# A longer prefix ahead of the branch: three graph attentions, group 0's first layer and all weight folding around the scan

## The chip, the cores and the metric

The kernel runs on one core of a Trainium2 chip. Its metric is device time in microseconds for one execution. Beside the runs there is a profiled execution, from which the views of the profile and the trace come; its span runs from the first to the last instruction. Engines are named as in the profile: PE is TensorE (PEld its weight loads), DVE is VectorE, ACT is ScalarE, POOL is GpSimd, SP is SyncE, which here issues the DMAs.

## The reference

128 graphs of 128 nodes with 256 features go through two layers. All arithmetic is in 32-bit floats.

```python
# layer 0: two graph attentions, then a feed-forward layer (256 -> 1024 -> 256)
def _gat(h, adj, W, a, out_features):
    Wh = jnp.matmul(h, W)
    Wh1 = jnp.matmul(Wh, a[:out_features])
    Wh2 = jnp.matmul(Wh, a[out_features:])
    e = jax.nn.leaky_relu(Wh1 + jnp.swapaxes(Wh2, 1, 2), negative_slope=ALPHA)
    scores = jnp.where(adj > 0, e, NEG)
    att = jax.nn.softmax(scores, axis=1)
    return jnp.matmul(att, Wh)
h = _gat(x, adj, W1, a1, Fout)
h = _gat(h, adj, W2, a2, W2.shape[1])
h = _layernorm(residual + h, g_ln1, b_ln1)
ff = jnp.matmul(jax.nn.relu(jnp.matmul(h, w_ff1) + b_ff1), w_ff2) + b_ff2
x = _layernorm(h + ff, g_ln2, b_ln2)
# layer 1: 8-head attention with a value matrix per relation r = 0..3, then a feed-forward layer
attn = softmax(q k^T / sqrt(dh))
for r in range(4):
    out = out + einsum('bhij,bhjd->bhid', attn * (adj == r), v_r)
x = _ln(src + out @ Wo + bo, g1, beta1)
ff = gelu(x @ W1 + b1) @ W2 + b2
return _ln(x + ff, g2, beta2)
```

## The kernel before, in words

The graphs are taken in 32 groups of four. Each group goes through five stages: `load` (features and mask), `gat` (both graph attentions), `ff0` (layer 0's feed-forward), `att` (layer 1's attention) and `ff1` (layer 1's feed-forward). Each stage is a Python generator that emits instructions and yields a planned time until its next piece; a heap in `layers` always continues the generator with the earliest planned time, so the pieces of several groups are mixed. `PERIOD` (100 units of plan) is the distance between groups, `begin` gives the start of each stage in a period, `early` moves single stages, and `times` holds the pauses. From a planned time on (`kept`), the order of emission is binding for TensorE and for SP; the other engines are ordered by the scheduler of the build.

Work differs by whether a group goes "direct". A transpose is either made by TensorE against the identity, into PSUM, and copied out (L282 to L286; L406 for the row of a graph attention), or by VectorE in blocks of 32 (L288) with a trip through DRAM that puts the blocks into place (four stores L291, one load L297; for a row L411 and L414). Direct is meant for groups with little other work beside them: before, the two graph attentions in the prefix, `ff0` of group 0, the features of `att` for group 0, and `ff0`, `att` and `ff1` of the last group. The weights of `att` for group 0 take the trip through DRAM (`turned`).

The names in the steps: L442 is x times the folded weights (wh), L450 and L461 the weighted sums of the first and second graph attention, L424 to L431 their softmax. L315 to L318 and L339 form the first feed-forward product from sums of blocks (seven products for eight), in two units of four visits each; L345 to L366 evict and activate; L384 is the second feed-forward product. L476 and L481 are q and k, L497 the scores, L501 to L513 the softmax over heads, L548 the values, L532 masks the weights, L563 weights the values, L590 is the product with Wo. `affine` (L271) applies a layer norm's gain and offset, `normalised` (L256 to L265) its mean and variance. `folded` (L184, L192, L195) multiplies a layer norm's gain into the next weights and its offset into their bias, `weight_sums` (L208 to L212) prepares the sums of weight blocks.

The program begins with a prefix. It loads the first weights and two groups, does these groups' graph attentions side by side, step by step, scans the whole adjacency input for a value above 1 (four parts of 2 MB, L722), folds wf1, and brings a flag to a register:

```python
        while gats:
            gats = [s for s in gats if next(s, None) is not None]
...
    with tc.If(found > 0) as arm:
        layers(tc, a, out, c, GENERAL)
    with arm.Else():
        layers(tc, a, out, c, BINARY)
```

With the inputs used the adjacency holds only 0 and 1, so the second arm runs (two value sets in place of four). All engines pass the branch. In the arm, group 0's attention stage first folds wq, wk, wv and w1; the graph attention of group 2 and everything later belongs to the arm.

## Time and profile before

| | us |
|---|---|
| median of 3 runs | 2838.19 (2837.97 to 2843.73) |
| profiled execution, its own time | 2833.85 |
| its span | 2831.9 |
| TensorE busy | 2718.5 |
| ScalarE busy | 1679.3 |
| GpSimd busy | 1547.0 |
| VectorE busy | 1527.5 |
| granted TensorE clock, mean | 0.982 |

Busy is the sum of the instructions' times on an engine. In the page's second part each digit is the busy share of one of 40 slices of the span in tenths; PEclk is the granted TensorE clock in tenths. In a table of windows the columns after a window are its length, then for each engine the busy time and the number of instructions, then the granted clock, the busy share of the DMA engines and the traffic. In a list of waits each line has the engine with the instruction that waited, what released it, the total in us, how many times, and the longest.

### The profile page before, as it was taken

What the parts mean: (1) busy time and instruction counts of PE and PEld (TensorE: products, weight loads), DVE (VectorE), ACT (ScalarE), POOL (GpSimd) and SP (SyncE); (2) the same over time, 40 slices, a digit from 0 to 9 for tenths busy, and PEclk for the clock granted to TensorE, in tenths of its full rate; (3) what the DMA queues carried; (4) which work ended last, traced back from release to release, by engine and by line L of the source; (5) the groups of instructions that cost most, each with busy time, mean ns of one, the idle gap of its engine ahead of it and who ended that gap; (6) DMA issues with size and microseconds to landing.
All of it is one profiled execution on the core that took longest, in us unless ns stands there. A gap on an engine that the chain in (4) does not pass through costs nothing.

```text
span 2831.9 us, 46682 instructions
## 1 busy us (share of the span) xinstructions
PE 2718.5 (96%) x16578; PEld 2148.2 (76%) x16578; DVE 1527.5 (54%) x2873; ACT 1679.3 (59%) x5063; POOL 1547.0 (55%) x1610
## 2 busy tenths in 40 slices
PE   4897999999999999999999999999999999999888
PEld 3775877777787777787777778778778877777766
DVE  5445555555654555565555555555556555555442
ACT  3445656666665666665666565566666556566443
POOL 1434646555655655665564565565566556556453
PEclk7898999999999999999999999999999999999999
DMA  7146365556456556555555655655664555565220
GB/s 281 46 100 143 83 134 112 111 128 142 105 115 133 112 107 139 118 120 121 119 113 119 142 108 113 137 109 108 135 133 108 118 124 117 110 142 108 63 51 15
DMA packets 1156945, 328.74 MB, mean 116 GB/s; under 512 B 903008, under 2 KB 1126752, under 8 KB 1156064
## 3 DMA queue, kind: packets, MB, share of 16 engines
q1 hardware_dynamic: 1156704, 325.68, 52.0%
q8 instruction: 133, 2.18, 0.3%
q14 instruction: 108, 0.88, 0.1%
HBM read 195.97 MB, written 129.62 MB: 115 GB/s over the span
## 4 chain that ended last, share of the span: by engine, by line
PE 62%; ACT 11%; DVE 10%; DMA 6%; POOL 5%; issue 4%; SPq 1%; ACTq 0%; DVEq 0%; POOLq 0%
PE mm L384 23%; PE mm L339 16%; PE mm L548 4%; PE mm L476 4%; DMA eT<-zd 4%; PE mm L481 4%; ACT e L510 3%; PE av L563 3%; ACT fT L360 2%; PE mm L590 2%; DVE nm L501 2%; ACT tok L265 2%; PE mm L497 2%; POOL e L513 2%; PE mm L450 2%
## 5 line engine op out<-in xcount | busy, mean ns | idle before, releaser
L271 POOL TENSOR_TENSOR tok<-tok,ln_rows 128x512 f32<-128x512 f32 x476 | 616.9, 1312 | 25.4 <-DVE T L288 8.1
L510 ACT ACTIVATE e<-mm,nm 128x128 f32<-128x128 f32 x1024 | 358.5, 402 | 203.9 <-DVE nm L501 201.5
L384 PE MATMUL mm<-w,fT 128*128 128x256 f32 x2048 | 463.8, 382 | 0.0
L384 PE MATMUL mm<-wf,fT 128*128 128x256 f32 x2048 | 448.7, 379 | 1.5 <-ACT fT L360 1.5
L384 PEld LDWEIGHTS mm<-wf,fT 128*128 128x128 f32 x2048 | 388.7, 190 | 55.4 <-ACT fT L360 1.9
L384 PEld LDWEIGHTS mm<-w,fT 128*128 128x128 f32 x2048 | 384.2, 190 | 59.4 <-issue 6.0
L532 DVE TENSOR_TENSOR m<-eT,am 128x1024 f32<-128x1024 f32 x128 | 183.9, 1437 | 404.6 <-DMA eT<-zd 403.9
L513 POOL TENSOR_TENSOR e<-e,s 128x1024 f32<-128x1024 f32 x128 | 254.4, 1994 | 133.7 <-DVE s L512 118.4
L265 ACT ACTIVATE tok<-tok,nmr,rstd 128x256 f32<-128x256 f32 x480 | 251.0, 608 | 117.9 <-POOL nmr L263 117.7
L431 POOL TENSOR_TENSOR e<-e,s 128x512 f32<-128x512 f32 (+1 forms) x68 | 68.0, 1000 | 455.7 <-DVE s L430 455.6
L315 POOL TENSOR_TENSOR t<-T 128x256 f32<-128x256 f32 x64 | 48.2, 753 | 450.9 <-DMA T<-zd 450.9
L429 ACT ACTIVATE e<-e,nm 128x128 f32<-128x128 f32 x256 | 99.6, 390 | 298.3 <-DVE nm L426 292.0
L510 ACT ACTIVATION_READ_ACCUMULATOR e<-mm,nm 128x1 f32 x1024 | 247.8, 242 | 0.0
L548 PE MATMUL mm<-wv,T 128*128 128x512 f32 x512 | 230.2, 592 | 0.0
L358 POOL TENSOR_TENSOR fT<-fT 128x512 f32<-128x512 f32 x128 | 161.1, 1269 | 86.7 <-ACT fT L357 86.6
L339 PE MATMUL mm<-T,wf 128*128 128x256 f32 x768 | 197.4, 381 | 0.0
L339 PE MATMUL mm<-T,w 128*128 128x256 f32 x768 | 194.4, 382 | 0.3 <-ACT T L286 0.2
L360 ACT ACTIVATE fT<-fT,col 128x512 f32<-128x512 f32 x256 | 167.8, 711 | 29.9 <-DVE fT L354 29.4
L256 DVE BATCH_NORM_STATS2 st<-tok 128x6 f32<-128x256 f32 x480 | 179.8, 412 | 4.1
L394 DVE TENSOR_TENSOR tok<-tok,mm 128x512 f32<-128x512 f32 x120 | 81.8, 681 | 182.7 <-PE mm L384 182.7
L339 PEld LDWEIGHTS mm<-T,w 128*128 128x128 f32 x768 | 147.1, 192 | 35.6 <-issue 15.5
L548 PEld LDWEIGHTS mm<-wv,T 128*128 128x128 f32 x512 | 97.1, 190 | 95.1 <-issue 87.5
(141 smaller groups left out, 5140.2 us busy)
## 6 DMA issues: line engine op xcount, KB each, us to landing
zd<-e SPq DMA_DIRECT2D x496, 128.0 KB, 3.6
eT<-zd SPq DMA_DIRECT2D x124, 512.0 KB, 5.1
zd<-T SPq DMA_DIRECT2D x364, 128.0 KB, 3.6
T<-zd SPq DMA_DIRECT2D x91, 512.0 KB, 4.4
xt<-in_xT_dram SPq DMA_DIRECT2D x32, 512.0 KB, 5.3
e<-zsd SPq DMA_DIRECT2D x60, 256.0 KB, 3.2
tok<-in_x_dram SPq DMA_DIRECT2D x30, 512.0 KB, 5.8
out_dram<-tok SPq DMA_DIRECT2D x29, 512.0 KB, 6.7
```

Of the source, the lines that this page charges most:

```text
L256: nc.vector.bn_stats(st, y[:, b])
L265: nc.scalar.activation(y[:, b], y[:, b], AF.Identity, bias=nmr[:, b:b + 1], scale=rstd[:, b:b + 1])
L271: engine.tensor_tensor(y[:, b:b + n], y[:, b:b + n], v[:, None, :].to_broadcast([P, n, D]), op)
L339: nc.tensor.matmul(p[:, i], win[k][:, ts(f0 + i, P)], hs[k], start=first and i == 0, stop=True, skip_group_check=True)
L358: nc.gpsimd.tensor_add(hi[:, :, 1], hi[:, :, 1], hi[:, :, 0])
L360: nc.scalar.activation(lo[:, i], lo[:, i], func, bias=bin_[:, f0 + i:f0 + i + 1])
L384: nc.tensor.matmul(ys[b // 2][:, b % 2], fT[f][:, ts(b, N)], wout[:, f], start=b % 2 == 0 and n == 0, stop=n == FC - 1, skip_group_check=True)
L476: nc.tensor.matmul(p, c.wq[:, f, ts(i, P)], hT[:, :, f], start=f == 0, stop=f == DC - 1)
L510: nc.scalar.activation(e[:, k], p[:, j, i], AF.Exp, bias=nms[q][:, j, i:i + 1], accum_out=s[:, k:k + 1])
L513: nc.gpsimd.tensor_mul(e, e, per_row(s, N))
L532: nc.vector.tensor_tensor(m, eT, at[:, b][:, None, :].to_broadcast([P, H, N]), OP.mult)
L548: nc.tensor.matmul(p, hT[:, b, f], wv[:, f, r:r + 2], start=f == 0, stop=f == DC - 1)
```

## The change

The prefix takes three groups through their graph attention (`LEAD` 3) and group 0 through `ff0` as well (`FIRST` 1), and does all folding of weights. It is emitted by the same heap as the arms, now a function `run`, with pauses of its own (`PREFIX`) and a binding order for TensorE and SP. The rows of the layer norms, wf2 and the buffers of weight sums move ahead of the scan; the sum of rows goes from VectorE to GpSimd. The scan is made in eight parts of 1 MB with four buffers (before four of 2 MB with three). In both arms `att` of group 0 is direct throughout, its weights included. In the arm for 0 and 1 some pauses and starts change, and the order is binding from planned time 120 in place of 280.

```diff
-LEAD = 2
+LEAD = 3
+FIRST = 1
+SCANS = 8
...
-        "wo": 12, "turned": 11, "next put": 2.5, "row put": 9, "affine": 9,
+        "sums": 6, ...
+        "next put": 2.5, "row put": 8, "affine": 13, "store": 21,
...
-    begin=dict(load=-96, gat=-61, ff0=45, att=129, ff1=303),
-    early={
-        (1, 'ff0'): 46,
-        (2, 'load'): 80,
-        (2, 'gat'): 80,
-        (2, 'ff0'): 80,
-        (3, 'load'): 5,
-        (-2, 'ff1'): -15,
-        (-1, 'load'): 5,
-    },
-    kept={PE: 280, SP: 0},
+    begin=dict(load=-96, gat=-61, ff0=47, att=129, ff1=303),
+    early={
+        (-2, "ff1"): -43, (-1, "load"): 5, (0, "att"): -5, (-1, "ff1"): 12, (-2, "att"): -6,
+        (-3, "att"): 2, (3, "ff0"): 2, (-4, "ff1"): 5, (4, "ff0"): 2,
+    },
+    kept={PE: 120, SP: 0},
...
+PREFIX = dict(TIMES, **{
+    "sums": 0.5, "ff visits": (1, 1, 2, 1, 0.5, 1, 1, 1), "ff2": 11, "ff first half": 0.5,
+    "ff half": 2, "row": 6, "gat": 12.5, "wh": 4.0, "put": 0.5, "lead ff0": 3.5, "scan": 7.5,
+    "scans": 25, "gats": (0, 12, 24), "fold": 24.5, "ffs": (48,), "second fold": 31.5,
+})
...
-        nc.vector.tensor_add(ln_rows[:, :3, 1], ln_rows[:, :3, 1], plus)
+    nc.gpsimd.tensor_add(ln_rows[:, :3, 1], ln_rows[:, :3, 1], plus)
...
-    def attention(y, g, first, direct):
-        hT = yield from features(y, first or direct)
+    def attention(y, g, direct):
+        hT = yield from features(y, direct)
...
-        if g == 0:
-            folded(nc, c, pools.ps, c.wq, c.col["bq"], "02")
-            folded(nc, c, pools.ps, c.wk, c.col["bk"], "02")
-            folded(nc, c, pools.ps, c.wv, c.bv, "02", rows=True)
...
-            folded(nc, c, pools.ps, c.w1, c.col["b1"], "11")
-            c.w1_sums = weight_sums(nc, c, c.w1, "w1")
-        x2[g] = yield from attention(x1.pop(g), g, g == 0, g == NG - 1)
+        x2[g] = yield from attention(x1.pop(g), g, alone(g))
...
+        def scan():
+            for k in range(SCANS // 2):
+                load(k)
+            others()
+            for k in range(SCANS):
+                yield PREFIX["scan"]
+                nc.vector.tensor_reduce(c.top[:, k:k + 1], chunks[k].bitcast(U32), AX.X, OP.max)
+                if len(chunks) < SCANS:
+                    load(len(chunks))
+
+        def gat(g):
+            ready[g] = yield from gat_block(True, f"wh{g}", g, c.xt[g], c.at[g], c.y[g])
+
+        def first_ff(g):
+            yield from ff0(ready.pop(g), True)
+
+        def fold():
+            folded(nc, c, pools.ps, c.wf1, c.col["bf1"], "01")
+            c.wf1_sums = weight_sums(nc, c, c.wf1, "wf1")
+            yield PREFIX["second fold"]
+            folded(nc, c, pools.ps, c.wq, c.col["bq"], "02")
+            folded(nc, c, pools.ps, c.wk, c.col["bk"], "02")
+            folded(nc, c, pools.ps, c.wv, c.bv, "02", rows=True)
+            yield 6
+            folded(nc, c, pools.ps, c.w1, c.col["b1"], "11")
+            c.w1_sums = weight_sums(nc, c, c.w1, "w1")
+
+        todo = [[PREFIX["gats"][g], 0, g, gat(g)] for g in range(LEAD)]
+        todo += [[PREFIX["ffs"][g], 1, g, first_ff(g)] for g in range(FIRST)]
+        todo += [[PREFIX["fold"], 2, 0, fold()], [PREFIX["scans"], 3, 0, scan()]]
+        run(tc, todo, {PE: (0, 1000), SP: (0, 1000)})
```

More of the change, by code (lines that the diff above doesn't have):

```diff
@@ L48 @@
     times=dict(TIMES, **{
-        "ff first half": 6, "ff half": 4, "row": 14.5, "wh": 3.5, "mask": 8.5, "av": 14.5,
-        "wo": 12, "turned": 11, "next put": 2.5, "row put": 9, "affine": 9,
-        "ff visits": (2.5, 2.5, 4, 4, 3.25, 3.25, 3.25, 3.25),
+        "sums": 6, "ff visits": (2.5, 2.5, 4, 4, 3.25, 3.25, 3.25, 3.25), "ff first half": 6,
+        "ff half": 4, "row": 14.5, "wh": 3.5, "mask": 8.5, "av": 14.5, "wo": 12, "turned": 11,
+        "next put": 2.5, "row put": 8, "affine": 13, "store": 21,
     }),
-    begin=dict(load=-96, gat=-61, ff0=45, att=129, ff1=303),
+    begin=dict(load=-96, gat=-61, ff0=47, att=129, ff1=303),
     early={
-        (1, 'ff0'): 46,
-        (2, 'load'): 80,
-        (2, 'gat'): 80,
-        (2, 'ff0'): 80,
-        (3, 'load'): 5,
-        (-2, 'ff1'): -15,
-        (-1, 'load'): 5,
+        (-2, "ff1"): -43, (-1, "load"): 5, (0, "att"): -5, (-1, "ff1"): 12, (-2, "att"): -6,
+        (-3, "att"): 2, (3, "ff0"): 2, (-4, "ff1"): 5, (4, "ff0"): 2,
     },
-    kept={PE: 280, SP: 0},
+    kept={PE: 120, SP: 0},
 )
+PREFIX = dict(TIMES, **{
[3 more added lines that the diff above has]
+})
 _COLS = {
@@ L113, in on_all_rows @@
         return bass.AP(tensor=v.tensor, offset=v.offset + first * D, ap=[[0, P], [1, n * D]])
-    c.xt, c.at = [], []
+    c.xt, c.at, c.top = [], [], tmp.tile([P, SCANS], F32, name="top")
     def load_group(g):
@@ L129, in constants @@
     load_mask(0)
-    load_group(1)
-    load_mask(1)
+    for g in range(1, LEAD):
+        load_group(g)
+        load_mask(g)
     pa = ps.tile([P, DC, 2], F32, name="mm")
@@ L143, in constants @@
         nc.vector.tensor_copy(c.wx[:, fc], p)
-    for g in range(LEAD):
-        nc.sync.dma_start(c.y[g], a["x"][g])
     col = cst.tile([P, a["cols"].shape[1]], F32, name="col")
@@ L150, in constants @@
     c.wf1 = wload("wf1")
-    def others():
-        ln_rows = cst.tile([P, len(KS), 2, D], F32, name="ln_rows")
-        nc.sync.dma_start(ln_rows, on_all_rows(0, 8))
-        plus = tmp.tile([P, 3, D], F32, name="plus")
-        nc.sync.dma_start(plus, on_all_rows(8, 3))
-        nc.vector.tensor_add(ln_rows[:, :3, 1], ln_rows[:, :3, 1], plus)
-        c.ln = {k: (ln_rows[:, n, 0], ln_rows[:, n, 1]) for n, k in enumerate(KS)}
-        c.wf2 = wload("wf2")
+    for g in range(LEAD):
+        nc.sync.dma_start(c.y[g], a["x"][g])
+    ln_rows = cst.tile([P, len(KS), 2, D], F32, name="ln_rows")
+    nc.sync.dma_start(ln_rows, on_all_rows(0, 8))
+    plus = tmp.tile([P, 3, D], F32, name="plus")
+    nc.sync.dma_start(plus, on_all_rows(8, 3))
+    nc.gpsimd.tensor_add(ln_rows[:, :3, 1], ln_rows[:, :3, 1], plus)
+    c.ln = {k: (ln_rows[:, n, 0], ln_rows[:, n, 1]) for n, k in enumerate(KS)}
+    c.wf2 = wload("wf2")
+    c.sums = {n: [cst.tile([P, c.FF // 2], F32, name=f"{n}s{i}") for i in (1, 2, 4)] for n in ("wf1", "w1")}
+    def others():
         c.wq = wload("wq")
@@ L168, in others @@
         c.w2 = wload("w2")
-        c.sums = {n: [cst.tile([P, w.shape[-1] // 2], F32, name=f"{n}s{i}") for i in (1, 2, 4)]
-                  for n, w in (("wf1", c.wf1), ("w1", c.w1))}
     return others
@@ L605, in stages_of @@
     return gat_block, ff0, attention, ff1, affine, load_group
-@with_exitstack
-def layers(ctx: ExitStack, tc: tile.TileContext, a: dict, out: bass.AP, c, plan: dict):
-    nc = tc.nc
-    NG = a["x"].shape[0]
-    TIMES, PERIOD = plan["times"], plan["period"]
-    pools = Pools(ctx, tc, plan["bufs"])
-    gat_block, ff0, attention, ff1, affine, load_group = stages_of(tc, a, out, c, pools, plan)
-    x0, x1, x2, loads = dict(enumerate(c.y)), {}, {}, {}
-    def stage_load(g):
-        loads[g] = load_group(g)
-        yield 1
-    def stage_gat(g):
-        x0[g] = yield from gat_block(False, "wh", g, *loads.pop(g))
-    def alone(g):
-        return g in (0, NG - 1)
-    def stage_ff0(g):
-        x1[g] = yield from ff0(x0.pop(g), alone(g))
-    def stage_attention(g):
-        if g == 0:
-            folded(nc, c, pools.ps, c.wq, c.col["bq"], "02")
-            folded(nc, c, pools.ps, c.wk, c.col["bk"], "02")
-            folded(nc, c, pools.ps, c.wv, c.bv, "02", rows=True)
-            if plan["binary"]:
-                D = c.D
-                nc.vector.tensor_sub(c.wv[:, :, D:2 * D], c.wv[:, :, D:2 * D], c.wv[:, :, :D])
-                nc.vector.tensor_sub(c.bv[:, D:2 * D], c.bv[:, D:2 * D], c.bv[:, :D])
-            folded(nc, c, pools.ps, c.w1, c.col["b1"], "11")
-            c.w1_sums = weight_sums(nc, c, c.w1, "w1")
-        x2[g] = yield from attention(x1.pop(g), g, g == 0, g == NG - 1)
-    def stage_ff1(g):
-        last = g == NG - 1
-        y = yield from ff1(x2.pop(g), last, 2 if last else G)
-        for b in range(0, G, 2):
-            if not last:
-                yield TIMES["affine"]
-            affine(y, "12", b, 2, nc.vector if last else nc.gpsimd)
-            if last:
-                nc.sync.dma_start(out[g][:, b:b + 2], y[:, b:b + 2])
-        if not last:
-            yield TIMES["store"]
-            nc.sync.dma_start(out[g], y)
-    make = dict(load=stage_load, gat=stage_gat, ff0=stage_ff0, att=stage_attention, ff1=stage_ff1)
-    early, todo = plan["early"], []
-    for g in range(NG):
-        for n, k in enumerate(STAGES):
-            if g >= LEAD or n > 1:
-                t = PERIOD * g + plan["begin"][k] - early.get((g, k), 0) - early.get((g - NG, k), 0)
-                todo.append([t, n, g, make[k](g)])
@@ L664, in layers, with run @@
+def run(tc, todo, kept):
+    traced = tc.nc.cur_bb.bb.instructions
     heapq.heapify(todo)
-    kept = {e: (since, PERIOD * NG + 60) for e, since in plan["kept"].items()}
-    traced = nc.cur_bb.bb.instructions
     last = {}
@@ L689, in graph_layers, with layers, stage_load, stage_gat @@
 @with_exitstack
+def layers(ctx: ExitStack, tc: tile.TileContext, a: dict, out: bass.AP, c, plan: dict):
+    nc = tc.nc
+    NG = a["x"].shape[0]
+    TIMES, PERIOD = plan["times"], plan["period"]
+    pools = Pools(ctx, tc, plan["bufs"])
+    gat_block, ff0, attention, ff1, affine, load_group = stages_of(tc, a, out, c, pools, plan)
+    x0, x1 = {g: c.y[g] for g in range(FIRST, LEAD)}, {g: c.y[g] for g in range(FIRST)}
+    x2, loads = {}, {}
+    def stage_load(g):
+        loads[g] = load_group(g)
+        yield 1
+    def stage_gat(g):
+        x0[g] = yield from gat_block(False, "wh", g, *loads.pop(g))
+    def alone(g):
+        return g in (0, NG - 1)
+    def stage_ff0(g):
+        x1[g] = yield from ff0(x0.pop(g), alone(g))
+    def stage_attention(g):
+        if g == 0 and plan["binary"]:
+            D = c.D
+            nc.vector.tensor_sub(c.wv[:, :, D:2 * D], c.wv[:, :, D:2 * D], c.wv[:, :, :D])
+            nc.vector.tensor_sub(c.bv[:, D:2 * D], c.bv[:, D:2 * D], c.bv[:, :D])
+        x2[g] = yield from attention(x1.pop(g), g, alone(g))
+    def stage_ff1(g):
+        last = g == NG - 1
+        y = yield from ff1(x2.pop(g), last, 2 if last else G)
+        for b in range(0, G, 2):
+            if not last:
+                yield TIMES["affine"]
+            affine(y, "12", b, 2, nc.vector if last else nc.gpsimd)
+            if last:
+                nc.sync.dma_start(out[g][:, b:b + 2], y[:, b:b + 2])
+        if not last:
+            yield TIMES["store"]
+            nc.sync.dma_start(out[g], y)
+    make = dict(load=stage_load, gat=stage_gat, ff0=stage_ff0, att=stage_attention, ff1=stage_ff1)
+    early, todo = plan["early"], []
+    for g in range(NG):
+        for n, k in enumerate(STAGES):
+            if n > 2 or g >= (FIRST if n == 2 else LEAD):
+                t = PERIOD * g + plan["begin"][k] - early.get((g, k), 0) - early.get((g - NG, k), 0)
+                todo.append([t, n, g, make[k](g)])
+    run(tc, todo, {e: (since, PERIOD * NG + 60) for e, since in plan["kept"].items()})
+@with_exitstack
 def graph_layers(ctx: ExitStack, tc: tile.TileContext, a: dict, out: bass.AP):
@@ L704, in graph_layers @@
     c.MW = D + 4
+    c.FF = a["wf1"].shape[1]
     cst = ctx.enter_context(tc.tile_pool(name="cst", bufs=1))
@@ L711, in graph_layers @@
         others = constants(tc, a, c, cst, tmp, pools.ps)
-        gat_block = stages_of(tc, a, out, c, pools, BINARY)[0]
-        gats = [gat_block(True, f"wh{g}", g, c.xt[g], c.at[g], c.y[g]) for g in range(LEAD)]
-        while gats:
-            gats = [s for s in gats if next(s, None) is not None]
-        words = a["adjT"].rearrange("g p b n -> (g p b n)").rearrange("(k p w) -> k p w", p=P, k=4)
-        top = tmp.tile([P, 4], F32, name="top")
-        for k in range(4):
-            t = tmp.tile([P, words.shape[2]], I32, name="scan", bufs=3)
-            nc.sync.dma_start(t, words[k])
-            nc.vector.tensor_reduce(top[:, k:k + 1], t.bitcast(U32), AX.X, OP.max)
@@ L723, in graph_layers, with load @@
-        others()
-        folded(nc, c, pools.ps, c.wf1, c.col["bf1"], "01")
-        c.wf1_sums = weight_sums(nc, c, c.wf1, "wf1")
+        gat_block, ff0 = stages_of(tc, a, out, c, pools, dict(BINARY, times=PREFIX))[:2]
+        words = a["adjT"].rearrange("g p b n -> (g p b n)").rearrange("(k p w) -> k p w", p=P, k=SCANS)
+        chunks, ready = [], {}
+        def load(k):
+            chunks.append(tmp.tile([P, words.shape[2]], I32, name="scan", bufs=SCANS // 2))
+            nc.sync.dma_start(chunks[k], words[k])
@@ L729, in graph_layers @@
         other = tmp.tile([P, 1], F32, name="other")
-        nc.vector.tensor_reduce(other, top, AX.X, OP.max)
+        nc.vector.tensor_reduce(other, c.top, AX.X, OP.max)
         nc.vector.tensor_scalar(other, other, 1.0, None, op0=OP.is_gt)
```

## The prediction

> **What bounds the kernel now.** I read the page first (parts 1 and 2), then cut the span into stages with the table of windows, then asked for TensorE's waits stage by stage, and last the timelines of all queues in the first 110 us, one period in the middle and the last 240 us.

> ```profile
> span 2831.9 us, 46682 instructions
> PE 2718.5 (96%) x16578; PEld 2148.2 (76%) x16578; DVE 1527.5 (54%) x2873; ACT 1679.3 (59%) x5063; POOL 1547.0 (55%) x1610
> ...
> PE   4897999999999999999999999999999999999888
> ...
> PEclk7898999999999999999999999999999999999999
> ```

> TensorE is the bound: 96% busy, no other engine above 59%. What can be won is its idle time, 2831.9 - 2718.5 = 113 us, and time at a low clock. Both lie at the two ends:

> ```profile
> core 0: us, PE busy (x) PEld busy (x) DVE busy (x) ACT busy (x) POOL busy (x), PEclk, DMA share, GB/s
> 0.00:72.70 72.70, 34.08 (x131) 27.66 (x131) 40.02 (x75) 22.48 (x73) 9.71 (x22) 0.71 0.72 274
> 72.70:300.00 227.30, 201.63 (x1150) 152.84 (x1151) 110.10 (x198) 113.35 (x360) 91.11 (x93) 0.93 0.42 90
> 300.00:2590.00 2290.00, 2275.11 (x14070) 1806.31 (x14070) 1279.04 (x2417) 1427.42 (x4309) 1326.10 (x1372) 1.00 0.56 121
> 2590.00:2831.90 241.90, 207.65 (x1231) 161.38 (x1229) 98.37 (x184) 116.09 (x321) 120.04 (x125) 0.93 0.23 51
> ```

> Idle: 38.6 us in the prefix (up to 72.7, TensorE's first instruction after the branch), 25.7 in the fill, 14.9 in the 2290 us of the steady part (0.65%), 34.3 at the end. Who is waited for in prefix, fill, end and (500 to 2500 us) steady part, in that order:

> ```profile
> PE mm L450 <- POOL e L431: 15.1, 3, 8.9
> PE mm L733 <- DVE other L731: 6.3, 1, 6.3
> PE mm L282 <- issue: 6.0, 1, 6.0
> ```
> ```profile
> PE av L563 <- DMA eT<-zd: 12.4, 4, 9.1
> ```
> ```profile
> PE mm L282 <- ACT tok L265: 12.1, 3, 5.3
> PE mm L590 <- ACT oT L567: 5.6, 1, 5.6
> PE mm L339 <- POOL t L315: 2.8, 1, 2.8
> ```
> ```profile
> PE mm L339 <- ACT fT L345: 9.4, 12, 1.8
> ```

> The prefix waits for two softmaxes with nothing beside them, for the scan and for the branch. The fill waits for group 0's weights on their way through DRAM (eT<-zd).

> [...] 8 instructions of L461 take 3.07 us in the prefix (6.14 for 16) and 1.89 in the middle. [...] flag written at 68.0, first TensorE instruction at 72.7, 4.7 us. [...] in the end stage 32 such transposes of e take 4.1 us, and each 128x512 copy 0.6.

> **The change, part by part.** Line numbers are those of the kernel before.

> *Work moved ahead of the branch*, at full clock: group 2's graph attention (L442 16 instructions 3.7, L450 8 in 1.9, L461 8 in 1.9 = 7.5 us), group 0's layer (8 transposes 1.5, L339 56 instructions 12.2, L384 64 in 13.9 = 27.6), folding of wq, wk, wv, w1 (0.95 + 1.03 + 3.6 + 3.7 = 9.3). Together **44.4 us** leave the fill.

> *How much longer the prefix gets.* I wrote down TensorE's new order, which is enforced from time 0, and walked it with the durations of the trace (ScalarE 0.38 a copy of wh, 0.27 a bias, 0.39 an exp with its sum; VectorE 0.34 a 256-wide step, 2.2 half an old scan part of 4.4; POOL 0.65 a weighting). The first loads and products are as before up to 12.2. Then three wh products with transposes between, and wf1's folding (3.5), keep TensorE busy to 27; group 0's first softmax is done at 23. First weighted sums of groups 0 and 1 and the rest of wh: to 37. Then a wait: two scan parts (4.4) stand in VectorE's queue ahead of group 0's second softmax; its weights come at 41: 4 us idle, then 3 at half clock, to 44. Then y0 has to be added and normalised (VectorE to 48, POOL 1.7, ScalarE behind four exps 3.1) before its transposes, and group 2's first weighted sum is queued behind these transposes: idle to 52, 8 us. From there group 0's layer, the folds and the last sums fill each other's gaps: group 2's sum 3.8 (half clock), transposes 1.7, evictions to 58, then 12.2 + 9.3 - 0.5 + 2 x 1.9 = 24.8 to 82, L384 to 96. Then adding, the last maximum, the flag matmul behind a normalisation on VectorE (3) and the branch (4.7): 104. Each of some twenty hand-overs between engines costs 0.1 to 0.2 that I left out, so I take **107** against 72.7: +34.3. The loads don't bind: 1.3 MB more for group 2 at some 400 GB/s are 3.3 us, wf1 lies 4.2 MB from the start of the queue (before 15 us), the scan's last four parts wait for buffers from 37, 39, 44 and about 54 us on, and behind them on SP there is only the flag. The sum of rows on POOL instead of VectorE (0.94; about 2 on POOL from L271's 1.3 for 512 columns) is queued ahead of group 1's weighting but its rows lie 7.2 MB in, some 20 us, before that is due at 27. Ends: 97 (no half clock, shorter waits) to 118 (the softmax chains as slow as before, where two took from 20 to 52).

> *After the branch.* Before, the fill from 72.7 to 300 lost 25.7 of idle and 8.3 of half clock (L442 6.0 for 3.7, L590 3.5 and 3.0 for 1.9 each, L563 4.3 for 1.9, L497 2.1 for 1.2): **34**. (The 6.0 of L282 <- issue lie ahead of 72.7 and are in the prefix.) It now starts with group 0's attention: transposes and their copies 1.6, half clock 2, kT 0.7, weights of the first pair 1.5 behind group 1's L339 (20 products cover 8.6 of the 11 us from scores to weights), activations 1, the second pair's weights 6 (as L590's and L282's waits in the end stage: 5.6 + 2.2), half clock again 1.5, group 1's features 1.5: **16**. Added on TensorE: 32 transposes 4.1 (group 2's 8, about 1.2, are in the walk). What goes: group 0's 16 stores and 4 loads by SP, and group 2's two row trips. Net -34 + 16 + 4 = **-14** (bounds -22 and 0). The direct copies of eT go to ScalarE and VectorE, 0.6 each for 8, both under 60% busy there.

> *The end.* The 30th group's last layer is put later and mixed with the 31st's: L282's wait of 5.3 gets other products ahead of it, and POOL t's 2.8 gets 13 L384 beside it. The other 4.2 + 2.6 + 5.6 + 2.2 keep their place in the order. -8, less 2 because L563 now follows only 5.3 us behind the last transposes of e: **-6** (bounds -12 and +4).

> *The steady part.* Its TensorE order differs only in that the second unit of L339 comes 8 L384 later, which gives L345's copies 3.5 us more: of 9.4 + 1.1 us I take **-3**. On SP the row put and the token load now stand ahead of both eT loads instead of between them; the trace has 8 us of slack there (second product m done at 1577.2, first L563 at 1585.5), so I cost it at nothing. If that cover is gone, L563 waits in each group. Bounds: -9 to +20.

> Sum: 34.3 - 44.4 - 14 - 6 - 3 = **-33 us**. Against the profiled execution's own 2833.85 (2831.9 of span) that is 2801; the median of the runs shown lies 4.3 higher at 2838.19, and from it 2805 follows, which I forecast.

> **The rivals.**
> (A) As worked out, with the branch anywhere from 100 to 114 and the end within 6 of its value: 2792 to 2818. For it: the idle time is there, and the moved work is at hand when TensorE stands. 60%.
> (B) The order stiffens the prefix. TensorE takes y0's transposes before group 2's ready sum, and the fill's new head behaves like the end stage. Prefix 118, 6 us more of waits, nothing from the end: 2805 + 11 + 6 + 6 = 2828. For it: VectorE is the busiest engine of the old prefix (40.0 of 72.7). 19%. Beyond A on the other side, prefix 97 and 12 us at the end, 2805 - 10 - 6 = 2789: 5%.
> (C) It does not do what it says: the waits just change places (prefix 118, no gain in the fill, end +4), 2805 + 11 + 14 + 10 = 2840, no change. A difference under 0.2%, 5.7 us, cannot be told from none. 5%.
> (D) Slower: a new wait in each period of the steady part, L563 for eT[...]. It decides from (33 + 5.7) / 29 groups = 1.3 us a group beyond the 8 us of slack; at 2 us a group, 2805 + 58 = 2863. For it: [...] the transfers take 4 to 5 us; against it: the slack, and only one L345 wait in that part today. 11%.

> **How the numbers follow.** Faster: A, B and the 5% below, 0.84. Same: C, 0.05. Slower: D, 0.11. The range of 2790 to 2834 reaches from the good end over A and B to the edge of C; D and most of C are left out, 15%.

> **What would show it.** Right: TensorE's first instruction after the branch between 100 and 114; about 40 more TensorE instructions (16618); PEclk above 0.8 in the first 100 us; 480 stores zd<-e and 120 loads eT<-zd; idle from the branch to 300 us at 10 to 20; the 5.3 of L282 gone. Wrong: a branch after 120, L563 <- DMA eT or L339 waits that come again in every period, or more than 35 us of idle after 2590.

## The result and the profile after

The changed kernel takes 2792.49 us (median of 4 runs, 2791.0 to 2793.45) where the kernel before, beside it, took 2838.08 (4 runs, 2833.25 to 2843.73): a ratio of 0.9838, 95% interval 0.9819 to 0.9857. The forecast was 2805, with a range of 2790 to 2834. The profiled execution takes 2792.19, its span 2790.4, which is 41.5 less than before. The medians differ by 45.6: the profiled execution of the kernel before (2833.85) was one of its faster ones.

The lines of the changed kernel carry mostly two more than those of the kernel before (L282 is now L284, L339 L341, L384 L386, L476 L478, L513 L515, L590 L592); the scan's maximum is L728, the flag matmul L760. All line numbers below are those of the kernel shown. Parts 1, 2 and 6 of the page of the changed kernel:

```profile
span 2790.4 us, 46726 instructions
PE 2714.0 (97%) x16618; PEld 2148.0 (77%) x16618; DVE 1507.7 (54%) x2882; ACT 1675.7 (60%) x5067; POOL 1569.2 (56%) x1613
...
PE   7889999999999999999999999999999999999988
...
PEclk8999999999999999999999999999999999999989
...
zd<-e SPq DMA_DIRECT2D x480, 128.0 KB, 3.5
eT<-zd SPq DMA_DIRECT2D x120, 512.0 KB, 5.2
```

The first slice was at 4 tenths and is at 7; TensorE is busy for 76% of the prefix (79.84 of 105.04 us) where it was for 47% (34.06 of 72.68). Instructions, stores and loads are the counts that the prediction named. TensorE's idle time went from 113.4 to 76.4 us (2790.4 - 2714.0), its busy time only from 2718.5 to 2714.0.

To see where, I cut both spans at the same points of the work: TensorE's first instruction after the branch, the first q product of group 4, and that of group 28. The table of windows of the kernel before, and then of the changed one (after the window: length, then busy time of TensorE, its weight loads, VectorE, ScalarE, GpSimd, the clock, the DMA share, GB/s):

```profile
0.00:72.68 72.68, 34.06 (x130) 27.64 (x131) 40.02 (x75) 22.48 (x73) 9.71 (x22) 0.71 0.72 274
72.68:442.66 369.98, 342.94 (x1996) 266.31 (x1997) 191.26 (x355) 202.24 (x618) 176.10 (x183) 0.96 0.47 102
442.66:2444.87 2002.21, 1989.31 (x12289) 1578.20 (x12288) 1119.23 (x2112) 1252.75 (x3792) 1161.74 (x1201) 1.00 0.56 121
2444.87:2831.90 387.03, 352.15 (x2165) 276.04 (x2163) 177.02 (x331) 201.87 (x580) 199.41 (x206) 0.96 0.35 77
```
```profile
0.00:105.04 105.04, 79.84 (x354) 65.52 (x355) 62.27 (x139) 44.83 (x134) 27.54 (x45) 0.85 0.54 202
105.04:421.24 316.20, 300.60 (x1812) 230.26 (x1813) 161.23 (x301) 179.06 (x561) 160.19 (x163) 0.97 0.46 99
421.24:2415.41 1994.17, 1986.57 (x12289) 1579.21 (x12288) 1111.96 (x2112) 1251.08 (x3792) 1181.47 (x1201) 1.00 0.56 121
2415.41:2790.40 374.99, 347.01 (x2165) 273.01 (x2163) 172.27 (x331) 200.77 (x580) 200.01 (x206) 0.96 0.36 80
```

The third and fourth rows have the same number of TensorE instructions in both kernels, so their differences are not differences of work. Prefix and fill together, where work only changes sides, are 21.4 us shorter (442.66 - 421.24), the steady part 8.0, the end 12.0. Idle time (length less busy time) fell by 24.9, 5.3 and 6.9; busy time rose by 3.4 in prefix and fill, where transposes were added, and fell by 2.7 and 5.1 in the other two, with the instructions equal.

Two causes of this fall can be read from the traces. In the steady part it is not the clock, which both traces record as full from one q product to the other (1.00 in both third rows). There, twelve L339 products that had waited for L345 kept TensorE busy for about 0.45 us each, where the same product in an unbroken row adds 0.22. No product of that place waits in the changed kernel, which accounts for the 2.7. At the end part of it is the clock: TensorE was busy at half clock for 19.0 us before and for 11.9 after. I estimate this at 3.5 of the 5.1 us, from eight products L452 that take 3.79 us in a stretch of half clock (27.68 in the changed kernel) and 1.91 at full clock (34.97).

What is still waited for, in the fill up to 300 us and in the last 200 us of the changed kernel (engine with the waiting instruction, what released it: total, times, longest):

```profile
PE mm L284 <- ACT y L267: 4.5, 1, 4.5
PE mm L284 <- POOL e L515: 4.0, 2, 3.2
PE mm L341 <- ACT fT L348: 2.6, 2, 1.3
PE mm L499 <- DVE T L479: 2.1, 1, 2.1
```
```profile
PE mm L592 <- ACT oT L569: 7.2, 1, 7.2
PE mm L284 <- POOL e L515: 3.9, 1, 3.9
PE mm L341 <- ACT fT L359: 2.5, 2, 2.1
PE mm L284 <- ACT tok L267: 1.4, 1, 1.4
```

The 4.5 on the first line are the branch: the flag matmul ends at 100.58, and TensorE's next instruction starts at 105.04. The 12.4 us for eT<-zd are gone (9.1 of them in one wait). At the end 1.4 us for the tokens are left of 12.1 (ACT tok, three waits before), and the 2.8 for POOL's t are gone. The 2.1 of L499 are new, and the last experiment is about them.

### The profile page after: what moved, and what is told of

It is laid out like the page before. It is cut to its first block, busy times and chain, and to the rows that moved or that the text cites. A ratio compares the mean times of both kernels' runs of the same rounds, so it can differ in the third digit from the quotient of the medians.

```text
span 2790.4 us, 46726 instructions
## 1 busy us (share of the span) xinstructions
PE 2714.0 (97%) x16618; PEld 2148.0 (77%) x16618; DVE 1507.7 (54%) x2882; ACT 1675.7 (60%) x5067; POOL 1569.2 (56%) x1613
## 4 chain that ended last, share of the span: by engine, by line
PE 73%; ACT 9%; DVE 8%; POOL 6%; issue 3%; DMA 1%; SPq 0%; ACTq 0%; DVEq 0%; POOLq 0%
PE mm L386 31%; PE mm L341 17%; PE mm L550 5%; PE av L565 4%; PE mm L478 4%; PE mm L483 4%; ACT fT L362 2%; PE mm L499 2%; ACT tok L267 2%; PE mm L452 2%; POOL e L515 2%; PE mm L592 2%; DVE nm L503 2%; POOL tok L273 2%; DVE st L258 2%
## 5 line engine op out<-in xcount | busy, mean ns | idle before, releaser
L273 POOL TENSOR_TENSOR tok<-tok,ln_rows 128x512 f32<-128x512 f32 x460 | 624.9, 1375 | 11.8 <-DVE T L290 3.5
L386 PE MATMUL mm<-w,fT 128*128 128x256 f32 x2048 | 465.1, 383 | 0.0
L386 PE MATMUL mm<-wf,fT 128*128 128x256 f32 x2048 | 448.2, 379 | 0.0
L386 PEld LDWEIGHTS mm<-w,fT 128*128 128x128 f32 x2048 | 385.3, 190 | 60.1 <-issue 6.5
L386 PEld LDWEIGHTS mm<-wf,fT 128*128 128x128 f32 x2048 | 389.4, 190 | 53.5 <-ACT fT L368 0.3
L515 POOL TENSOR_TENSOR e<-e,s 128x1024 f32<-128x1024 f32 x128 | 241.8, 1896 | 246.5 <-DVE s L514 131.8
L317 POOL TENSOR_TENSOR t<-T 128x256 f32<-128x256 f32 x64 | 53.9, 842 | 537.2 <-DMA T<-zd 534.5
L534 DVE TENSOR_TENSOR m<-eT,am 128x1024 f32<-128x1024 f32 x128 | 175.7, 1375 | 332.2 <-DMA eT<-zd 331.9
L267 ACT ACTIVATE tok<-tok,nmr,rstd 128x256 f32<-128x256 f32 x464 | 242.8, 610 | 165.0 <-POOL nmr L265 150.2
L550 PE MATMUL mm<-wv,T 128*128 128x512 f32 x512 | 234.4, 601 | 0.0
L419 ACT ACTIVATE e<-e,wh 128x128 f32<-128x128 f32 x232 | 74.1, 390 | 228.9 <-DMA e<-zsd 228.9
L341 PE MATMUL mm<-T,w 128*128 128x256 f32 x768 | 192.3, 379 | 1.2 <-ACT fT L354 1.2
L341 PE MATMUL mm<-T,wf 128*128 128x256 f32 x768 | 192.7, 379 | 0.0
L503 DVE TENSOR_REDUCE nm<-mm 128x4 f32<-128x512 f32 x256 | 163.6, 681 | 30.9 <-PE mm L499 30.9
L258 DVE BATCH_NORM_STATS2 st<-tok 128x6 f32<-128x256 f32 x464 | 173.2, 411 | 3.0
L550 PEld LDWEIGHTS mm<-wv,T 128*128 128x128 f32 x512 | 98.9, 194 | 97.7 <-issue 87.1
```

Of the source, the lines that this page charges most:

```text
L258: nc.vector.bn_stats(st, y[:, b])
L267: nc.scalar.activation(y[:, b], y[:, b], AF.Identity, bias=nmr[:, b:b + 1], scale=rstd[:, b:b + 1])
L273: engine.tensor_tensor(y[:, b:b + n], y[:, b:b + n], v[:, None, :].to_broadcast([P, n, D]), op)
L341: nc.tensor.matmul(p[:, i], win[k][:, ts(f0 + i, P)], hs[k], start=first and i == 0, stop=True, skip_group_check=True)
L386: nc.tensor.matmul(ys[b // 2][:, b % 2], fT[f][:, ts(b, N)], wout[:, f], start=b % 2 == 0 and n == 0, stop=n == FC - 1, skip_group_check=True)
L503: nc.vector.tensor_reduce(nm.rearrange("p j i -> p (j i)"), p.rearrange("p j i n -> p (j i) n"), AX.X, OP.max, negate=True)
```

## Experiments

In the expectations N is the reading of the traces above: each part of the change brings its gain at its own place, and the parts add up. M is the rival, worded for each run: the part brings nothing where it is made, or what it wins is made up for elsewhere. All are made from the changed kernel unless said otherwise. Spans and stage times come from the one profiled execution of each, medians from 4 runs, which spread by 1.8 to 10.5 us, so a difference of 2 or 3 us of span is near what can be told apart; "q4" and "q28" are the first q products of groups 4 and 28.

| kernel | branch | q4 | q4 to q28 | rest | span | median |
|---|---|---|---|---|---|---|
| before | 72.7 | 442.7 | 2002.2 | 387.0 | 2831.9 | 2838.08 |
| changed | 105.0 | 421.2 | 1994.2 | 375.0 | 2790.4 | 2792.49 |
| e1 old pauses | 104.5 | 422.9 | 2007.1 | 387.5 | 2817.5 | 2818.75 |
| e2 old shifts at the end | 104.9 | 420.8 | 1997.4 | 384.2 | 2802.4 | 2806.25 |
| e3 group 0's weights through DRAM | 105.2 | 414.8 | 1995.1 | 376.5 | 2786.4 | 2789.28 |
| e4 before, with new pauses and shifts | 72.8 | 444.8 | 1995.9 | 375.3 | 2816.0 | 2815.37 |
| e5 folds back in the arm | 101.5 | 424.8 | 1995.9 | 377.3 | 2798.0 | 2799.35 |
| e6 first layer back in the arm | 81.9 | 432.0 | 1993.6 | 375.1 | 2800.8 | 2803.6 |
| e7 group 2's sum ahead of y0 | 100.4 | 408.9 | 1996.9 | 373.3 | 2779.2 | 2780.68 |
| e8 scan later | 102.7 | 417.7 | 1995.2 | 374.5 | 2787.3 | 2787.15 |
| e9 = e3 + e7 | 101.5 | 412.4 | 1994.9 | 374.7 | 2782.0 | 2783.57 |
| e10 = e3 + e7 + e8 | 103.7 | 415.1 | 1995.6 | 374.1 | 2784.7 | 2786.55 |
| e11 = e7 + e8 | 102.1 | 409.3 | 1995.6 | 376.3 | 2781.2 | 2783.53 |
| e12 one eviction to ScalarE | 104.0 | 412.3 | 1997.1 | 373.0 | 2782.4 | 2787.3 |

### e1_old_pauses: the steady part's pauses taken back

```diff
-        "sums": 6, ... "next put": 2.5, "row put": 8, "affine": 13, "store": 21,
+        ... "next put": 2.5, "row put": 9, "affine": 9, ...
-    begin=dict(load=-96, gat=-61, ff0=47, att=129, ff1=303),
+    begin=dict(load=-96, gat=-61, ff0=45, att=129, ff1=303),
```

> The changed kernel with the old pauses and the old start of ff0 in the arm (sums 5, row put 9, affine 9, store 25, ff0=45); prefix, group 0's attention and the end's shifts stay. Theory N (the new pauses alone make the steady part faster: the second unit's first products come after 8 more L386, so that the copies L347 are done): the distance of two groups, 83.1 us in the changed kernel, goes back to 83.4, the span gets 8 us longer (2798), the waits of L341 for the copies of L347/L348 come back with about 9 us, and prefix and end are as in the changed kernel. Rival M (the steady part is faster because the groups enter it in another alignment, set by prefix and fill): distance stays at 83.1 and the span within 2 us of 2790.4.

(The pauses `sums` and `store`, which are no longer named, fall back to 5 and 25.)

Measured: span 27.1 longer. The steady part is 12.9 longer, and 12.5 are lost at the end, where N expected no change. TensorE's waits in the steady part and, below, the largest at the end:

```profile
PE mm L341 <- ACT fT L347: 10.5, 13, 1.8
```
```profile
PE mm L463 <- POOL e L433: 6.5, 1, 6.5
```

The direction is N's, the size well above its figure: with the old pauses and the new shifts the second weighted sum of a late group comes 6.5 us too early for its softmax. The pauses are a part of the gain both in the steady part and at the end.

### e2_old_end: the shifts at the end taken back

```diff
-        (-2, "ff1"): -43, (-1, "load"): 5, (0, "att"): -5, (-1, "ff1"): 12, (-2, "att"): -6,
-        (-3, "att"): 2, (3, "ff0"): 2, (-4, "ff1"): 5, (4, "ff0"): 2,
+        (-2, "ff1"): -15, (-1, "load"): 5, (0, "att"): -5, (3, "ff0"): 2, (4, "ff0"): 2,
```

> The changed kernel with the old shifts of the last groups ((-2, ff1): -15 and (-1, load): 5 only). Theory N: the 12 us that the last four groups gained come from putting the 30th group's last layer later; the waits of 5.3 us of L284 for tok L267 and of 2.8 for the sums t come back, span +8 to +12 us (2798 to 2802). Rival M (the end is shorter because the steady part hands over the groups in another alignment): +0 to +3 us.

Measured: span 12.0 longer, 9.2 of it at the end (N). Waits of the kernel before are back in the list for the end (8.5 of the 12.1 us for tokens), one line number lower than in the changed kernel:

```profile
PE mm L283 <- ACT tok L266: 8.5, 3, 4.2
...
PE mm L340 <- POOL t L316: 2.8, 1, 2.8
```

The column "rest" shows that pauses and shifts work only together at the end: 387.0 with both old, 384.2 with new pauses alone (e2), 387.5 with new shifts alone (e1), 375.0 with both.

### e4_before_new_plan: the kernel before, with the new pauses and shifts

```diff
-        ... "next put": 2.5, "row put": 9, "affine": 9, ...
+        "sums": 6, ... "row put": 8, "affine": 13, "store": 21,
-    begin=dict(load=-96, gat=-61, ff0=45, att=129, ff1=303),
+    begin=dict(load=-96, gat=-61, ff0=47, att=129, ff1=303),
...
-        (-2, 'ff1'): -15,
-        (-1, 'load'): 5,
+        (-2, 'ff1'): -43, (-1, 'load'): 5, (-1, 'ff1'): 12, (-2, 'att'): -6, (-3, 'att'): 2, (-4, 'ff1'): 5,
```

> The kernel before with nothing changed but the plan of the arm: new pauses, ff0=47 and the new shifts of the last groups; prefix, fill and group 0's attention are the old ones. Theory N (the parts add up): steady part -8 and end -12, so 2812 of span against 2831.9 and 2818 in time against 2838. Rival M (alignment from the prefix makes these gains): -5 us or less, or a loss.

Measured: span 15.9 shorter than before, ratio 0.9928 (0.9911 to 0.9944): -6.3 in the steady part, -11.7 at the end, +2.1 at the start. With these two edits alone, steady part and end are within 2 us of the changed kernel's. So of the 41.5 us the plan of pauses and shifts brings some 18 to 20, and the rest of the change 21.4 in prefix and fill. The next two runs undo two parts of that rest; the third graph attention, the scan in eight parts and the order that binds from 120 were not undone alone.

### e5_folds_in_arm and e6_no_first_ff: parts of the prefix taken back

e5 moves the folding of wq, wk, wv and w1 back to the start of `stage_attention` of group 0; e6 leaves `ff0` of group 0 to the arm and, as before the change, starts that of group 1 46 units early:

```diff
-        if g == 0 and plan["binary"]:
+        if g == 0:
+            folded(nc, c, pools.ps, c.wq, c.col["bq"], "02")
+            ...
+            c.w1_sums = weight_sums(nc, c, c.w1, "w1")
```
```diff
-FIRST = 1
+FIRST = 0
-        (-2, "ff1"): -43, (-1, "load"): 5, (0, "att"): -5, (-1, "ff1"): 12, (-2, "att"): -6,
+        (-2, "ff1"): -43, (-1, "load"): 5, (0, "att"): -5, (1, "ff0"): 46, (-1, "ff1"): 12, (-2, "att"): -6,
```

> The changed kernel with the folding of wq, wk, wv and w1 back in group 0's attention stage of the arm, all else as changed. Theory N (moving work pays only where it fills a gap; in the changed prefix these 9.3 us of TensorE stand where group 0's layer alone would wait for its evictions): the branch comes 4 to 7 us earlier (98 to 101 in place of 105), the fill gets 9 to 14 us longer because group 0's q and k wait behind folding and scaling; span +3 to +10 us. Rival M (TensorE is full there, work moved is neutral): branch 9 us earlier, fill 9 us longer, span within 2 us of 2790.4.

> The changed kernel with group 0's layer 0 feed-forward back behind the branch (FIRST = 0, and group 1's 46 units early again, as before the change); three graph attentions and all folding stay in the prefix. Theory N (group 0's layer is what fills the waits of the prefix): its 27.6 us of TensorE leave the prefix, which gets only 15 to 22 us shorter (branch at 83 to 90), and the fill takes 27 us and more waits for copies and features: span +6 to +16 us. Rival M (it is the early start of the graph attentions that pays): branch 27 us earlier, span within 3 us.

Measured: e5 has its branch only 3.5 us earlier, for 9.3 us of folds taken out, and its span is 7.6 longer; e6 has it 23.1 us earlier for 27.6 us of work, and its span is 10.4 longer. In span it is N in both; the branch of each lies at or just outside the edge of N's figure (98 to 101, and 15 to 22 us earlier). Both prices may be too low by some 4 to 5 us, because neither kernel has the loss in the fill that e12 isolates below (from group 2's q product to group 4's 167.8 and 166.3 us, against 171.4 in the changed kernel). What the folds filled is seen in the timeline of TensorE in e5 (start, us, engine, line, shapes, count, in brackets the idle time ahead and its releaser), where group 1's second weighted sum now waits:

```profile
76.47 3.54 PE L463 MATMUL mm<-wh,e 128*128 128x256 f32 x8 [5.05 <-POOL e L433]
```

The folds cost the prefix only 3.5 us, the other 5.8 lay in gaps such as this one. Group 0's layer was not: of its 27.6 us only 4.5 lay in gaps, and the rest of its gain (10.4 - 4.5) comes after the branch: group 0's q product stands 2.8 us behind the branch in the changed kernel and 58.5 in e6.

### e3_group0_dram: group 0's weights through DRAM again

```diff
-    def attention(y, g, direct):
-        hT = yield from features(y, direct)
+    def attention(y, g, first, direct):
+        hT = yield from features(y, first or direct)
...
-        x2[g] = yield from attention(x1.pop(g), g, alone(g))
+        x2[g] = yield from attention(x1.pop(g), g, g == 0, g == NG - 1)
```

> The changed kernel with the weights of group 0's attention again on the trip through DRAM (its features stay on TensorE). Theory N (the direct path is worth it because the fill has too little other work to hide the trip): 32 transposes (4.1 us) and their waits for the weights (L284 for L515, 4.0 us) go, but L565 waits for eT again, about 9 us in the second pair as before, and half clock follows: span +3 to +8 us. Rival M (with three groups and layer 0 of group 0 ahead, the fill has work enough, and the direct path only adds TensorE work): -4 to -8 us.

Measured: 4.0 us shorter, against N. N's wait was also of another kind than expected: no L565 waits for eT, but group 1's features now come late on their own trip (T<-zd), and two other products wait:

```profile
168.14 6.63 PE L478 MATMUL mm<-T,wq 128*128 128x512 f32 x8 [3.69 <-DMA T<-zd]
185.83 2.07 PE L341 MATMUL mm<-T,wf 128*128 128x256 f32 x4 [5.89 <-DMA T<-zd]
```

I read the shorter span at first as proof that group 0's direct transposes don't pay in the new fill. e9 to e12 speak against that.

### e7_sum_before_y0 and e8_scans_later: the two waits of the prefix

In the timeline of TensorE in the changed kernel the two waits that the prediction's walk foresaw stand at 39 to 42 and at 46 to 52 us:

```profile
41.86 3.78 PE L463 MATMUL mm<-wh,e 128*128 128x256 f32 x8 [3.11 <-POOL e L433]
51.90 2.17 PE L284 MATMUL mm<-ident,y 128*128 128x128 f32 x8 [6.25 <-ACT y L267]
```

e7 starts `ff0` of group 0 later, which puts group 2's first weighted sum (L452) ahead of y0's transposes; e8 starts the scan's maxima later, so that they don't stand in VectorE's queue ahead of group 0's second softmax:

```diff
-    "scans": 25, "gats": (0, 12, 24), "fold": 24.5, "ffs": (48,), "second fold": 31.5,
+    "scans": 25, "gats": (0, 12, 24), "fold": 24.5, "ffs": (51.5,), "second fold": 31.5,
```
```diff
-    "scans": 25, "gats": (0, 12, 24), "fold": 24.5, "ffs": (48,), "second fold": 31.5,
+    "scans": 44, "gats": (0, 12, 24), "fold": 24.5, "ffs": (48,), "second fold": 31.5,
```

> The changed kernel with group 0's layer planned at 51.5 instead of 48 in the prefix, so that TensorE takes group 2's first weighted sum (L452) ahead of the transposes of y0. Theory N (those transposes hold back work that is ready, the walk's 8 us, 6.3 measured): the wait of L284 for y L267 shrinks from 6.3 to about 2.5, the branch comes 3 to 5 us earlier, span 2785 to 2788. Rival M (y0 and the softmax of group 2 behind it set the end of the prefix, not TensorE's queue): the wait moves behind the transposes, branch and span within 1.5 us.

> The changed kernel with the scan planned to start at 44 instead of 25: its parts leave VectorE's queue ahead of the second softmaxes and go behind group 0's evictions. Theory N (two parts of 2.2 us delay group 0's second softmax): the wait of L463 for e (3.1 us) goes, the branch comes 2 to 4 us earlier unless the last parts end behind L386. Rival M (the scan's last parts and their loads become the end of the prefix): the flag matmul waits over 5 us for VectorE in place of 2.3, span +1 to +6 us.

Measured, e8: the 3.1 us of L463 are gone, but the flag matmul waits 4.4 in place of 2.3 for the scan's end; the branch is 2.3 earlier, the span 3.1 shorter. e7: the sum fills the wait, as its timeline of TensorE shows,

```profile
44.41 2.81 PE L452 MATMUL mm<-wh,e 128*128 128x258 f32 x8
50.87 2.16 PE L284 MATMUL mm<-ident,y 128*128 128x128 f32 x8 [3.64 <-ACT y L267]
```

and the branch comes 4.6 us earlier, as N said (the wait shrinks to 3.6, not to 2.5). But the span is 11.2 shorter, more than N or M allowed: e7 is the fastest kernel of this study, 2780.68, ratio 0.9805 to before (0.9786 to 0.9824). Some 6.6 us more came from after the branch, though the plan of the arm is the same in both kernels: 3.1 between the branch and group 2's q product, 4.6 between that and group 4's, less 1.1 given back later. That was open.

### e9, e10 and e11: do the savings add up?

These are e3 and e7 together, the same with e8's edit, and e7 with e8's edit (the diffs are those above).

> The changed kernel with group 0's weights back on the trip through DRAM and group 2's first weighted sum ahead of y0's transposes. If both savings are their own (theory N), they add up: span 2790.4 - 4.0 - 11.2 = 2775 (2773 to 2778), TensorE's first instruction after the branch at 100 to 101, first q product of group 4 at 402 to 405. If they come from one and the same place, the fill between 240 and 420 us that got smoother by chance in each (theory M), the second one brings only its prefix part: 2779 - 1 = 2777 to 2783, first q product of group 4 at 407 to 412.

> The run before with the scan's first maximum at planned time 44 in place of 25. Theory N (each shortens the prefix for itself): the 3.1 us of the second weighted sum go too, branch at 98 to 99, span 2.3 to 3.1 below the run before, 2771 to 2774. Theory M (the scan then ends the prefix): the flag matmul's wait grows from about 2 to 5 or more, branch at 100 to 102, span within 1.5 of the run before.

> The changed kernel with group 2's first weighted sum ahead of y0's transposes and the scan's first maximum at 44; group 0's weights stay direct. Theory N: 2779.2 - 3 = 2776 (2775 to 2778), branch at 98 to 99. Theory M (the scan ends the prefix): branch at 100 to 102, span 2778 to 2782.

Measured: they don't add up. e9 is 2.8 us longer than e7, M's outcome and at its far end; so e3 and e7 had both removed one and the same loss. With the loss gone, the trip through DRAM costs 2.8 us of span (e9 against e7) and 3.5 (e10 against e11), in the medians 2.9 and 3.0. Group 0's direct weights seem to pay, then, and in e3 that price was hidden behind the loss that the edit happened to remove. The size is not certain: from the branch to q4 the price is 2.5 and 4.2 us, the runs of e10 and e11 overlap, and the stages behind differ by up to 2 us between kernels with one and the same plan there.

e8's edit brings nothing on top of e7: the spans of e10 and e11 are 2.7 and 2.0 longer than those of e9 and e7, and their branches later, at 103.7 and 102.1, beyond what either theory said for e10. The scan's last maximum on VectorE ends at 96.1 us in e10 and at 88.8 in e9. So the flag matmul, which in e9 follows L386 without a wait, waits in e10, though for 2.5 us and not for the 5 or more that M named:

```profile
98.92 0.19 PE L760 MATMUL mm<-ones,other 128*1 128x1 f32 x2 [2.51 <-DVE mv L259]
```

### e12_q_on_scalar: one instruction of VectorE

The common loss lies between the first q products of groups 2 and 4: 171.4 us in the changed kernel, 166.2 to 166.8 in e3 and e7, 166 to 168 in e5, e6 and e8 to e11. It was 167.1 in the kernel before, so the loss is new. (e1 and e2 have 178 and 173; e1 loses there to other waits.) In the timeline of VectorE the changed kernel has this order,

```profile
252.77 0.75 DVE L479 TENSOR_SCALAR T<-mm,col 128x512 f32<-128x512 f32 x1 [5.33 <-PE mm L478]
259.35 1.22 DVE L534 TENSOR_TENSOR m<-eT,am 128x1024 f32<-128x1024 f32 x1 [5.83 <-DMA eT<-zd]
260.49 0.74 DVE L479 TENSOR_SCALAR T<-mm,col 128x512 f32<-128x512 f32 x1
```

where the masking of the weights of the group before (L534), for which VectorE waits 5.8 us until its DMA has landed, stands ahead of the second eviction of q. TensorE's scores (L499) wait 2.1 us for that eviction. The same order is found in e2, where L498 waits 4.0 us for it, and in none of the others made from the changed kernel (e1, e3 and e5 to e11): there both evictions stand ahead of both maskings. In this trace the second eviction, whose product ended at about 254.4 (L478, on TensorE from 249.82 for 4.62), ran only at 260.49, 1.14 us after the start of the masking ahead of it. VectorE's order isn't bound by `kept`, it is the build's choice, and as the runs show a change elsewhere can tip it. e12 moves that one eviction to ScalarE:

```diff
-            nc.vector.tensor_scalar(qT[:, i], p, c.col["bq"][:, i:i + 1], SCALE, op0=OP.add, op1=OP.mult)
+            if g == 2 and i == 1:
+                bqs = wk.tile([P, 1], F32, name="bqs", bufs=1)
+                nc.scalar.mul(bqs, c.col["bq"][:, i:i + 1], SCALE)
+                nc.scalar.activation(qT[:, i], p, AF.Identity, bias=bqs, scale=SCALE)
+            else:
+                nc.vector.tensor_scalar(qT[:, i], p, c.col["bq"][:, i:i + 1], SCALE, op0=OP.add, op1=OP.mult)
```

> The changed kernel with one instruction moved: the second eviction of group 2's q product (L479) goes from VectorE, where it stands behind a masking of weights (L534) that waits for the eT load of the group before, to ScalarE, with the scale folded into its bias. All five orders are otherwise those of the changed kernel. Theory N (this place on VectorE is what makes the stretch from the q product of group 2 to that of group 4 171.4 us long where seven other variants need 166 to 168): L499's wait of 2.1 us goes, and with the half clock that follows it the stretch falls to 167 to 169.5, span 2786.5 to 2788.5. Rival M (the two waits of L341 for fT just ahead of it, 2.7 us, and the clock lost by them are the cause, the eviction only shows there): L499's wait goes, but the stretch stays at 170 to 171.4 and the span at 2789 to 2791.

Measured: the stretch takes 166.25, N and a little more. Rival M's two waits ahead of q are there in e12 as well (1.2 and 1.5 us), so they are not the cause. The timelines of TensorE, of the changed kernel and of e12 (where L499 is L504), show what one late eviction costs:

```profile
261.29 1.35 PE L499 MATMUL mm<-kT,T 32*128 32x128 f32 x26 [2.12 <-DVE T L479]
262.57 8.62 PE L386 MATMUL mm<-w,fT 128*128 128x256 f32 x32
```
```profile
253.87 1.17 PE L504 MATMUL mm<-kT,T 32*128 32x128 f32 x32
254.97 7.17 PE L386 MATMUL mm<-w,fT 128*128 128x256 f32 x32
```

From the first score to the end of these 32 products the changed kernel takes 12.45 us (258.67 to 271.12), e12 8.21 (253.87 to 262.08): 4.2 us, half of it the wait of 2.1 and half slower products, most of them at the half clock that the trace records from 262.12 to 265.53. Another 1.0 of the stretch is the q product itself, 4.62 against 3.60: in the changed kernel half clock is recorded at its start (248.47 to 251.88), in e12 not, though the waits ahead are the same two. The median is 5.2 us below the changed kernel's; the profiled execution is 8.0 below, but it is the fastest of e12's 4 runs (2784.24 to 2790.39), so I rely on the 4.2. From the branch to group 2's q product e12 is 2.8 us shorter than the changed kernel, before the moved eviction can act, and 2.6 of this is busy time of the same instructions. I put these down to the clock: in the two parts of that stretch, up to and from group 1's q product, it was 0.90 and 0.99 in the changed kernel and 0.93 and 1.00 in e12 (last section).

## Why the prediction was right, and where its sizes were off

*The prefix.* +34.3 was predicted, +32.4 measured (72.68 to 105.04). The walk in TensorE's enforced order held at its milestones: group 0's wait 3.1 us for the 4 predicted, y0's wait 6.25 for 8 and ending at 51.9 for 52, the last product L386 done at 98.1 for 96. Both waits are what the walk said they were: e8 removes the first by moving the scan, e7 shortens the second by putting a ready sum ahead. Two of the walk's inputs can be set beside the trace of the kernel before: of the hand-overs in its prefix L431 to L450 takes 0.05 us, L426 to L429 0.10 and L430 to L431 0.02 to 0.19 (my estimate was 0.1 to 0.2), and the DMAs moved 352 to 430 GB/s from 5 to 30 us (400 taken). The 2.1 at the last milestone are nearly the price of a half clock that the walk had not counted, behind the folding of w1 (1.3 for L463, 0.6 for L386; last section). So the sum for a prefix that had never run was good to 2 us: its order was known, and its durations had rows in the trace of the kernel before.

*Moved work and fill.* Idle time from the branch to 300 us is 15.25 (a window of 194.96 with 179.71 busy), 10 to 20 was predicted. The fill's -14 came out as -9.4 up to group 4 (from branch to q4, 369.98 - 316.20 = 53.8 less the 44.4 moved). The term that was too good is the end of the fill: I had no new waits after group 1, and one arose at 258 us, from VectorE's unbound order, worth 4.2 with its low clock (e12). Taking those out, -13.6. The direct path was counted as a gain, which e3 alone would have denied and e9 to e11 support, at about 3 us.

*The steady part.* -8.0, predicted -3. The order was as said: the second unit of L339 comes later. The step that failed is the size, "of 9.4 + 1.1 us I take -3". The 3.5 us that L345's copies were to gain are more than the longest wait for them (1.8), and all of those waits went. In the list for this part stand 6.2 us for L359's copies, 14 waits, and nothing else; between the same two q products it was 9.1 for L345 and 1.0 for L357 before. Idle time fell by 5.3. The other 2.7 came as busy time, with the same 12,289 instructions, from the products that had stood behind those waits; my sum had no line for that. e4 (-6.3) and e1 (+12.9) show that the pauses do it; which of them, no run separates.

*The end.* -12.0, predicted -6, and at the edge of its bound. Two things failed. The waits of 4.2 and 2.6 for tokens, of which I wrote that they "keep their place in the order", went as well (12.1 of tok before, 1.4 in the last 200 us now); the 7.2 of L592 and the 3.9 of e are in place of 5.6 and 2.2. And 5.1 us of busy time went with the waits, some 3.5 of them at half clock, which my sum had no line for. e2 and e1 show that shifts and pauses are both needed for it.

*The rivals.* D, the new wait in each period behind the row put, did not occur: no wait of L565 for eT is in the list of the steady part. B had the two prefix waits' nature right, but they ended in time. The forecast lay 12.5 above the result. The 5 and 6 missing in the last two terms and 1.9 in the prefix, less the 4.6 lost in the fill, are 8.3 of it. Nearly all the rest is the median, which I had put 4.3 above the profiled execution as it was before; the changed kernel's median lies 0.3 above its own.

That the result lies inside the range is in part luck. It is 2.5 above the low end, the end of the kernel is at the edge of what A allowed, and the gains that were put too low are in part made up by a loss that nobody planned: e12, which takes that loss away with one instruction, has a median of 2787.3, below the range. The mechanism holds part by part; the sum of sizes held with the help of errors that go against each other.

## What to carry to other kernels

Where an engine's order is bound and every duration has a row in the trace, walk the new order instruction by instruction: here that gave a stage that had never run to within 2 us. Price a removed wait together with what follows it, the restart and the clock (behind L499's wait of 2.1 us another 2.1), and look for the queue whose order is nobody's choice: one instruction waiting for a DMA ahead of another engine's input cost 4.2 us here and probably made a useful edit look harmful. Before an edit is judged by undoing it alone, undo it beside a second version of the kernel: the same edit measured -4.0 in one and +2.8 and +3.5 in two others.

## What the hardware did that I had not expected

The clock after a wait is not the same each time. After almost the same two waits for e (3.2 and 0.8 us in the changed kernel, 3.2 and 0.5 in e12) the eight value products L550 took 5.71 us in the changed kernel and 3.85 in e12, 3.60 at full clock elsewhere. The granted clock shows the difference: half clock for 6.83 us in the changed kernel (first line), for 3.41 in e12 (second).

```profile
166.55:173.38 6.83, 6.07 (x14) 3.45 (x14) 5.39 (x6) 0.82 (x2) 3.26 (x3) 0.50 0.90 197
```
```profile
164.94:168.35 3.41, 2.89 (x13) 2.33 (x12) 2.10 (x3) 1.16 (x2) 3.33 (x3) 0.50 0.69 201
```

The clock also fell where TensorE was busy throughout. Behind 32 folding products of one column, in the changed kernel without any idle time, half clock is recorded from 81.22 to 84.63, and L463 takes 3.21 us in place of 1.89:

```profile
77.14 3.63 PE L194 MATMUL mm<-col,w 128*128 128x1 f32 x32
80.63 3.21 PE L463 MATMUL mm<-wh,e 128*128 128x256 f32 x8
```

The products behind such folds are slow in the variants too. The eight L452 behind wf1's fold take 3.46 to 3.79 us in the changed kernel and in all eleven made from it (1.91 at full clock). The next eight products behind w1's fold (L463 or L341) take 2.46 to 3.76 us in the changed kernel and in the ten that have this fold in the prefix (1.89 at full clock). Why the clock falls there is not shown. What remains open is what put ScalarE's evictions (L354, L359) late just ahead of the q product of group 2, where L341 waits 1.2 and 1.5 us in the changed kernel and in e12 but not in e7.
